# One pack of h, transposed through DRAM and in squares of 32 instead of by TensorE, in a two-layer graph kernel

## The chip, the cores and the metric

The kernel runs on one core of a Trainium2 chip. A core has five engines with queues of their own: TensorE (PE in the profile; its weight loads are listed apart as PEld), VectorE (DVE), ScalarE (ACT), GpSimd (POOL) and SyncE (SP). Here SP and ACT issue the DMAs, and sixteen DMA engines carry them. The metric is device time in microseconds, the median of several executions; lower is better. Kernel before: 2154.19 us, the median of three runs from 2152.48 to 2154.23.

## The reference: what is computed

`x` is 3327 x 512 and `adj` 3327 x 3327, all float32. Two layers follow each other, each with a residual:

```
h = relu(layernorm(x))
q, k, v = h @ Wq.T + bq, h @ Wk.T + bk, h @ Wv.T + bv
x = x + softmax(q @ k.T / sqrt(512) + adj + adj) @ v

h = relu(layernorm(x))
A2 = adj + I;  d = diag(A2) ** -0.5
x = x + relu((d[:, None] * A2 * d[None, :]) @ (A2 @ h @ W.T))
```

The kernel pads the rows to 3328, which is 26 tiles of 128 rows.

## The kernel before, in words

Queries and keys are never made apart. `Wq` and `Wk` are multiplied into one 512 x 512 matrix `M`, the first layer's scores are `h` times `M` times `h` transposed, and every large product is done as a product of 2 x 2 blocks with seven multiplications in place of eight. So TensorE needs `h` transposed, with the 512 features on the partitions, and it needs it as seven left factors: A11, A12, A22 and four sums S1 to S4.

**The packs.** The 26 row tiles are 13 pairs: tile t of the upper half and tile t of the lower half of the rows. `PACKS` (L204) divides the pairs into four packs, of 4, 3, 3 and 3 pairs, and `TURN` (L205) sets the order in which they are prepared: pack 1, 2, 0, 3. "The third pack" is pack 0: four pairs, eight tiles, 512 columns per half. `hp[k]` (L208) holds pack k: for each of the seven factors two chunks of 128 features by n x 128 columns. The upper half of the rows gives A11 (feature chunks 0 and 1) and A12 (chunks 2 and 3); the lower half gives A21 and A22, of which A21 goes only into the sums S1 = A22 + A21 and S3 = A11 + A21. S2 = S1 + A11, and S4 = A12 + S2.

**How a pack is turned.** There are two ways in the kernel before.

- `h_transposed` (L295 to L316), for the first three packs in that order. For each tile: load of 128 rows of `x` (L266), statistics on VectorE (L185 to L195) with a power on GpSimd (L191), normalisation and relu on ScalarE into a tile `ht` (L302), a store of `ht` to DRAM by rows for later use (L303), four 128 x 128 transposes on TensorE into PSUM (L306), and the way out of PSUM: one copy on ScalarE for an upper tile (L309), or a copy on ScalarE and two additions on VectorE for a lower tile (L311 to L313). At the end of a pack there are two wide additions (L315, L316).
- `Turned` (L324 to L381), for the fourth pack only. It loads the pack from a transposed copy of `x` in DRAM (L356) and applies mean and scale there; the means and scales come by way of six-row transposes on TensorE (L343), a small store (L346) and two broadcast loads (L360). The second of these loads goes into buffer `half1`.

**Rings of buffers.** `ht` comes from a ring of four buffers (`n_ring`, L262), `xt` from a ring of eleven (L261). The transposes go through two PSUM banks (L220, `tp_bank`).

**The products.** `project_q(k)` (L383) multiplies pack k by `M`: two chains (`o` = 0, 1) of seven products each. A chain (`Chain`, L222) issues m1, p5, p2, p6, then p4 of the chain before, p3, p7; its own p4 waits until the next chain. m1 reads A11, p5 reads S1, p2 reads A12, p6 reads S2, p3 reads S4, p7 reads S3, p4 reads A22. A product is two matmuls, which the profile lists as four. ScalarE (L403) and VectorE (L407) gather them into `qs`, and SP stores `qs` to DRAM (L415). After four of the seven products something else can be put beside (`place`, L391), counted from `late` on.

**What sets the order.** Within this first part of the kernel each engine's order is planned by the framework's scheduler, by the order in the program and by its own estimate of when inputs are ready. Only inside `in_order(...)` (L112) does an engine keep the order of the program among the instructions written there. Before, that is VectorE's order during the products of the third and fourth pack (L462 to L467). SP issues its DMAs one after the other, and a DMA that waits holds back all that are behind it in SP's order.

After this part come the scores (L542 to L588), the attention and the second layer (L935 above all), all tied to TensorE.

At the end of the kernel the same two building blocks that the change uses are at work already, on other data: `x1c` is filled by DMAs in runs of 128 bytes (L1154 to L1161), and VectorE transposes in squares of 32 (L1169).

Of the kernel before, what the change touches and what calls it, by code (L numbers as in the profile page):

```python
# [10 lines left out]
F32 = mybir.dt.float32  # L11
AF = mybir.ActivationFunctionType
# [3 lines left out]
P = 128  # L16
BW = 512
# [18 lines left out]
HALF = 13  # L36
# [7 lines left out]
ROW = tuple(STRIPS[s] + y * HT[s] + k for y in range(2) for s in range(2) for k in range(HT[s]))  # L44
# [3 lines left out]
def graph_layers_kernel(  # L48
# [30 lines left out]
    nc = tc.nc  # L79
    NP, D = x.shape  # L80
    DC = D // P
    NT = NP // P
    scale = 1.0 / math.sqrt(D)
# [11 lines left out]
    def half(k, shape, name):  # L95
        return arena.tile(shape, F32, name=name, tag=f"half{k}")
# [31 lines left out]
    dram = ctx.enter_context(tc.tile_pool(name="dram", bufs=1, space=bass.MemoryType.DRAM))  # L128
# [53 lines left out]
    def norm(src, kept=None):  # L182

        st = small.tile([P, 6], F32, name="st")
        nc.vector.bn_stats(st, src)  # L185
        mv = small.tile([P, 2], F32, name="mv") if kept is None else kept
        nc.vector.bn_aggr(mv, st)
        ve = small.tile([P, 1], F32, name="ve")
        nc.vector.tensor_scalar(ve, mv[:, 1:2], EPS, None, op0=ALU.add)  # L189
        rstd = small.tile([P, 1], F32, name="rstd") if kept is None else kept[:, 1:2]  # L190
        nc.gpsimd.tensor_tensor(rstd, ve, mhalf, op=ALU.pow)  # L191

        def bias():
            nb = small.tile([P, 1], F32, name="nb")
            nc.vector.scalar_tensor_tensor(nb, mv[:, 0:1], -1.0, rstd, op0=ALU.mult, op1=ALU.mult)  # L195
            return nb

        return rstd, bias
# [23 lines left out]
    class Chain:  # L222
# [7 lines left out]
        def __init__(self, product, first, more, last):  # L230


            X, Y, Z = x_bank("X"), y_bank("Y"), z_bank("Z")
            product(Y, "m1", True)
            first(0, Y, -1)
            product(Z, "p5", True)
            first(3, Z, -1)
            product(X, "p2", True)
            more(0, X)
            product(Y, "p6", False)  # L240
            first(1, Y, -1)
            Chain.finish()
            product(Z, "p3", False)
            more(1, Z)
            product(Y, "p7", False)
            more(3, Y)

            def rest():
                product(Y, "p4", False)
                first(2, Y, 1)  # L250
                last()

            Chain.before = rest
# [10 lines left out]
    def load_x(i, queue=nc.sync):  # L264
        xt = x_ring([P, D], "xt")
        queue.dma_start(xt, x[ROW[i] * P : (ROW[i] + 1) * P])  # L266
        return xt
# [27 lines left out]
    def h_transposed(k, tp_bank=tp_bank):  # L295

        a, n = PACKS[k]
        for _, i in (o for o in order if o[0] == k):
            xt = first.pop(i) if i in first else load_x(i)
            rstd, bias = norm(xt)  # L300
            ht = n_ring([P, D], "ht")
            nc.scalar.activation(ht, xt, AF.Relu, bias=bias(), scale=rstd)  # L302
            nc.sync.dma_start(rowd[0][ROW[i]], ht)  # L303
            pt = tp_bank("tp").rearrange("p (c e) -> p c e", c=DC)
            for c in range(DC):
                nc.tensor.transpose(pt[:, c], ht[:, c * P : (c + 1) * P], ident)  # L306
            w = slice((i % HALF - a) * P, (i % HALF - a + 1) * P)
            if i < HALF:
                nc.scalar.copy(hp[k][:, 0:2, :, w], pt.rearrange("p (a c) e -> p a c e", a=2))  # L309
            else:  # L310
                nc.scalar.copy(hp[k][:, 2, :, w], pt[:, 2:4])  # L311
                nc.vector.tensor_add(hp[k][:, 3, :, w], hp[k][:, 2, :, w], pt[:, 0:2])
                nc.vector.tensor_add(hp[k][:, 5, :, w], hp[k][:, 0, :, w], pt[:, 0:2])  # L313
            yield
        nc.vector.tensor_add(hp[k][:, 4], hp[k][:, 3], hp[k][:, 0])  # L315
        nc.vector.tensor_add(hp[k][:, 6], hp[k][:, 1], hp[k][:, 4])  # L316

    def after(ins, other):
# [2 lines left out]
                          mybir.DependencyInfo(mybir.DependencyClass.NoSync, mybir.DependencyReason.DATA),  # L321
                          reason="in_order")

    class Turned:  # L324


# [12 lines left out]
        def turn(self):  # L339
            k, stats, n = self.k, self.stats, PACKS[self.k][1]  # L340
            pt, by_row = tp_bank("tp"), half(3, [P, P], "by_row")
            for m in range(2):
                nc.tensor.transpose(pt[: 2 * n, m * P : (m + 1) * P], stats[:, m], ident)  # L343
                rows = by_row[32 * m : 32 * m + 2 * n]
                nc.scalar.copy(rows, pt[: 2 * n, m * P : (m + 1) * P])
                nc.sync.dma_start(normd[k][m][0, : 2 * self.w].rearrange("(i p) -> i p", p=P), rows)  # L346

        def load(self):
            k, w = self.k, self.w
            self.other = half(2, [P, 2, BW], "a21")[:, :, :w]  # L350
            a11, a12, a22 = hp[k][:, 0], hp[k][:, 1], hp[k][:, 2]
            for y, blocks in enumerate(((a11, a12), (self.other, a22))):
                c0 = ROW[y * HALF + PACKS[k][0]] * P
                xs = xT[:, c0 : c0 + w].rearrange("(z c p) e -> z p c e", z=2, p=P)
                for z, to in enumerate(blocks):
                    after(nc.sync.dma_start(to, xs[z]), self.row)  # L356
            self.norms = []
            for m in range(2):
                self.norms.append(half(m, [P, 2, BW], "norms")[:, :, :w])
                self.loaded = nc.sync.dma_start(  # L360
                    self.norms[m], normd[k][m][0:1, : 2 * w].rearrange("a (y e) -> a y e", y=2).to_broadcast([P, 2, w]))

        def parts(self):
            o, (a11, a12, a22, s1, s2, s3, s4) = self.other, (hp[self.k][:, j] for j in range(7))
            mean, by = ([e[:, y : y + 1].to_broadcast([P, 2, self.w]) for y in range(2)] for e in self.norms)
            nc.gpsimd.tensor_sub(a11, a11, mean[0])
            nc.gpsimd.tensor_sub(a12, a12, mean[0])

            def scaled(v, y):
                return nc.vector.scalar_tensor_tensor(v, v, 0.0, by[y], op0=ALU.max, op1=ALU.mult)  # L370

            yield nc.vector.tensor_sub(a22, a22, mean[1])
            yield scaled(a22, 1)
            yield nc.vector.tensor_sub(o, o, mean[1])
            yield scaled(o, 1)
            yield nc.vector.tensor_add(s1, a22, o)
            yield scaled(a11, 0)
            yield nc.vector.tensor_add(s2, s1, a11)
            yield scaled(a12, 0)
            yield nc.vector.tensor_add(s4, a12, s2)  # L380
            yield nc.vector.tensor_add(s3, a11, o)  # L381

    def project_q(k, beside=iter(()), late=0):  # L383
        a, n = PACKS[k]
        w = n * P

        qs = [half(8 + j, [P, 2, BW], "qs") for j in range(4)]

        places = itertools.count()

        def place():  # L391
            if next(places) >= late:
                next(beside, None)

        def chain(o):
            def product(ps, name, start):
                for c in range(2):
                    nc.tensor.matmul(ps[:, :w], M[B[name]][:, c, o * P : (o + 1) * P], hp[k][:, A[name], c],  # L398
                                     start=start and c == 0, stop=c == 1, skip_group_check=True)

            def first(j, ps, sign):
                d = 2 * (j % 2) + o
                nc.scalar.activation(qs[j][:, o, :w], ps[:, :w], AF.Identity, bias=u[:, d : d + 1], scale=float(sign))  # L403
                place()

            def more(j, ps):
                nc.vector.tensor_add(qs[j][:, o, :w], qs[j][:, o, :w], ps[:, :w])  # L407
                place()

            def last():  # L410
                if o == 1:
                    for j in range(4):
                        y, z = divmod(j, 2)
                        i = ROW[y * HALF + a] * P
                        ins = nc.sync.dma_start(qd[:, 2 * z : 2 * z + 2, i : i + w], qs[j][:, :, :w])  # L415
                        if behind:
                            after(ins, behind[-1])

            Chain(product, first, more, last)

        for o in range(2):
            chain(o)
# [29 lines left out]
        nc.tensor.matmul(pu[:, r : r + 1], weighed[:, r * P : (r + 1) * P], ones, start=True, stop=True)  # L452
    nc.vector.tensor_scalar(u, pu[:, :DC], scale, None, op0=ALU.mult)
    behind = []
    for then in TURN[1:3]:
        for _ in h_transposed(then):
            pass
        project_q(TURN[TURN.index(then) - 1])
    fourth = Turned(TURN[3])
    fourth.turn()  # L460
    fourth.load()
# [1291 lines left out]
```

## Time and profile before

| what | value |
|---|---|
| median of three runs | 2154.19 us |
| the profiled execution's own time | 2153.03 us |
| its span, first to last instruction | 2151.2 us |
| TensorE busy | 2137.8 us, 99% of the span |
| VectorE busy | 1653.9 us, 77% |
| ScalarE busy | 273.0 us, 13% |
| 16 DMA engines, mean over the span | 275 GB/s |
| mean granted TensorE clock | 0.998 of full speed |

The profile is of one execution. Times in it count from the start of the span. A matmul's record can overlap the next one's; the chain of work counts each stretch once. Idle time is put down to the event that ended it.

### The profile page before, as it was taken

To read this page: it belongs to the slowest core of one execution; us is meant where nothing else is said; L and a number is where in the kernel's file an instruction comes from. 1 tells how busy PE (TensorE), PEld (TensorE's weight loads), DVE (VectorE), ACT (ScalarE), POOL (GpSimd) and SP (SyncE) were. 2 spreads that over 40 slices of the span, in tenths; PEclk is the share of its full clock that TensorE was granted. 3 is DMA by queue.
4 is the path that set the end of the run, shared out by engine and by line. 5 is a ranking of instruction groups with operands and counts; after the bars stand their busy time and mean duration, and the time that the engine had idled before them with its cause. 6 is when DMAs were issued, how large, how long until landed. Compare 5 with 4: busy or idle time off the path is not lost.

```text
span 2151.2 us, 20908 instructions
## 1 busy us (share of the span) xinstructions
PE 2137.8 (99%) x6272; PEld 1182.0 (55%) x6272; DVE 1653.9 (77%) x3235; ACT 273.0 (13%) x441; POOL 68.7 (3%) x63
## 2 busy tenths in 40 slices
PE   9999999999999999999999999999999999999998
PEld 5555555555555555555454555555666665555554
DVE  7479888888997688776777778887576666778887
ACT  5312221112110000001111000000111100000000
POOL 2000000000004000000111000000000000000000
PEclk9999999999999999999999999999999999999999
DMA  8678888888999899888788889986646578978996
GB/s 301 215 241 301 303 307 286 307 293 284 328 338 293 292 370 333 280 304 304 264 304 263 308 276 369 322 310 222 198 156 209 151 219 246 313 223 245 269 288 177
DMA packets 402498, 592.10 MB, mean 275 GB/s; under 512 B 139964, under 2 KB 273480, under 8 KB 402376
## 3 DMA queue, kind: packets, MB, share of 16 engines
q1 hardware_dynamic: 374056, 532.72, 75.2%
q10 hardware_dynamic: 28320, 57.95, 7.4%
q8 instruction: 52, 0.85, 0.2%
q14 instruction: 70, 0.57, 0.1%
HBM read 422.71 MB, written 173.87 MB: 277 GB/s over the span
## 4 chain that ended last, share of the span: by engine, by line
PE 94%; DVE 3%; DMA 2%; issue 0%; ACT 0%; SPq 0%; ACTq 0%; DVEq 0%
PE p L935 55%; PE Y L542 13%; PE Z L542 6%; PE p L926 5%; PE p L1042 4%; PE pw L1103 4%; PE X L542 3%; PE Y L398 2%; PE Z L398 1%; DMA part<-sum 1%; PE X L398 1%; DMA xt<-in_x_dram 0%; DMA p<-s 0%; PE tp L306 0%; DVE g L546 0%
## 5 line engine op out<-in xcount | busy, mean ns | idle before, releaser
L935 PE MATMUL p<-part,b 128*128 128x448 f32 (+1 forms) x3528 | 1257.6, 513 | 0.3 <-DVE part L165 0.2
L935 PEld LDWEIGHTS p<-part,b 128*128 128x128 f32 x3528 | 669.9, 190 | 541.7 <-issue 290.4
L542 PE MATMUL Y<-qt,hp 128*128 128x448 f32 (+1 forms) x832 | 308.2, 513 | 0.2 <-DVE g L546 0.2
L164 DVE TENSOR_TENSOR part<-part 128x896 f32<-128x896 f32 (+1 forms) x252 | 256.8, 1019 | 65.0 <-DMA part<-p 26.2
L542 PEld LDWEIGHTS Y<-qt,hp 128*128 128x128 f32 x832 | 157.8, 190 | 133.7 <-issue 72.7
L542 PE MATMUL Z<-qt,hp 128*128 128x384 f32 (+1 forms) x416 | 162.2, 512 | 0.0
L166 DVE TENSOR_TENSOR part<-part,part 128x448 f32<-128x448 f32 (+1 forms) x219 | 129.5, 591 | 15.0
L165 DVE TENSOR_TENSOR part<-part,part 128x448 f32<-128x448 f32 (+1 forms) x219 | 129.4, 591 | 7.3
L926 PE MATMUL p<-part,b 128*128 128x448 f32 (+1 forms) x336 | 124.2, 512 | 0.0
L542 PEld LDWEIGHTS Z<-qt,hp 128*128 128x128 f32 x416 | 79.0, 190 | 66.2 <-issue 37.9
L546 DVE SCALAR_TENSOR_TENSOR g<-g,Y 128x384 f32<-128x384 f32 (+1 forms) x156 | 91.5, 587 | 30.0 <-PE Y L542 26.5
L978 ACT COPY part<-p 128x384 f32<-128x384 f32 (+1 forms) x33 | 16.6, 503 | 657.1 <-PE p L935 551.2
L926 PEld LDWEIGHTS p<-part,b 128*128 128x128 f32 x336 | 63.8, 190 | 54.1 <-issue 31.2
L549 ACT ACTIVATE g<-g 128x768 f32<-128x768 f32 (+1 forms) x48 | 43.0, 896 | 345.6 <-DVE g L546 288.0
L542 PE MATMUL X<-qt,hp 128*128 128x384 f32 (+1 forms) x208 | 81.1, 512 | 0.0
L979 DVE TENSOR_TENSOR part<-p,part 128x384 f32<-128x384 f32 (+1 forms) x33 | 19.3, 586 | 66.0 <-PE p L935 65.2
L1042 PE MATMUL p<-w,ct 128*128 128x512 f32 x136 | 61.6, 592 | 0.0
L542 PEld LDWEIGHTS X<-qt,hp 128*128 128x128 f32 x208 | 39.5, 190 | 33.1 <-issue 19.3
L191 POOL TENSOR_TENSOR rstd<-ve,mhalf 128x1 f32<-128x1 f32 x46 | 38.9, 847 | 530.6 <-DVE ve L189 502.1
L998 DVE TENSOR_TENSOR ct<-p,part 128x448 f32<-128x448 f32 (+1 forms) x72 | 42.3, 609 | 16.1 <-PE p L926 12.0
L1103 PE MATMUL pw<-w,rows 128*128 128x256 f32 x208 | 53.4, 379 | 0.0
L1033 DVE TENSOR_TENSOR job<-job 128x896 f32<-128x896 f32 (+1 forms) x52 | 52.9, 1018 | 0.0
(194 smaller groups left out, 1683.5 us busy)
## 6 DMA issues: line engine op xcount, KB each, us to landing
part<-sum SPq DMA_DIRECT2D x104, 448.0 KB, 5.0
part<-p SPq DMA_DIRECT2D x91, 448.0 KB, 5.9
part<-sum SPq DMA_DIRECT2D x104, 384.0 KB, 4.1
part<-p SPq DMA_DIRECT2D x91, 384.0 KB, 4.3
part<-in_adjT_dram SPq DMA_DIRECT2D x78, 448.0 KB, 5.1
b<-row SPq DMA_DIRECT2D x234, 128.0 KB, 4.8
part<-in_adjT_dram SPq DMA_DIRECT2D x78, 384.0 KB, 3.8
g<-in_adjT_dram SPq DMA_DIRECT2D x52, 448.0 KB, 4.2
```

Of the source, the lines that this page charges most:

```text
L164: yield nc.vector.tensor_add(o[:, 0:2], g[:, 0:4:3], g[:, 1:2].to_broadcast([P, 2, g.shape[-1]]))
L165: yield nc.vector.tensor_add(o[:, 2], o[:, 1], g[:, 0])
L166: yield nc.vector.tensor_add(o[:, 3], o[:, 2], g[:, 2])
L398: nc.tensor.matmul(ps[:, :w], M[B[name]][:, c, o * P : (o + 1) * P], hp[k][:, A[name], c], start=start and c == 0, stop=c == 1, skip_group ...
L542: nc.tensor.matmul(ps[:, :wd], h_of(self.t, name, k), qt[B[name]][:, k], start=start and k == 0, stop=k == 1, skip_group_check=True)
L546: nc.vector.scalar_tensor_tensor(a[n], a[n], 2.0, ps[:, :wd], op0=ALU.mult, op1=ALU.add if sign > 0 else ALU.subtract)
L549: nc.scalar.activation(g[1], g[1], AF.Exp, **({"bias": pad} if self.t == HALF - 1 else {}))
L926: yield nc.tensor.matmul(ps[("p2", "p3", "p4", "p8")[k]][:, :w], b[:, z], a[:, 0, y], start=k == 3 and not self.seeded, stop=True, skip_gr ...
L935: yield nc.tensor.matmul(ps[r][:, :w], b[:, i], m, start=self.t == 0 and not adds, stop=self.t == PAIRS - 1 and r in ("p1", "p5", "p6", "p ...
L1033: nc.vector.tensor_add(self.a, self.a, self.b)
L1042: nc.tensor.matmul(ps, cts[s][y][d][:, k * P : (k + 1) * P], w[d], start=d == 0, stop=d == DC - 1)
L1103: nc.tensor.matmul(ps, a, W[B[name]][:, c], start=new and c == 0, stop=c == 1, skip_group_check=True)
```

## The change

The third pack is no longer turned by `h_transposed`. A new class `Blocked` normalises its eight tiles as before, all four upper tiles first and then the lower four. It stores each `ht` twice: by rows as before, and by chunks of 128 features into a new DRAM tensor `by_chunk`. It then loads `by_chunk` back so that 128-byte runs (32 floats) of 32 rows land on 32 partitions: four loads for the upper half, eight for the lower half. After that each square of 32 x 32 still has to be transposed, which VectorE does in place, and four wide additions make the sums. The third pack's A21 is kept in the buffer `half1`. The program's order changes too: `project_q(TURN[0])` now stands before the third pack's preparation, and VectorE's share of that preparation is put beside the products of the second pack from the ninth place on (`late` is 8), in a fixed order on VectorE.

```diff
+    class Blocked:
+        def __init__(self, k):
+            self.k, (a, n) = k, PACKS[k]
+            self.rows = [dram.tile([DC, n * P, P], F32, name=f"by_chunk{y}") for y in range(2)]
+            for y in range(2):
+                for t in range(n):
+                    i = a + t + y * HALF
+                    xt = first.pop(i) if i in first else load_x(i)
+                    rstd, bias = norm(xt)
+                    ht = n_ring([P, D], "ht")
+                    nc.scalar.activation(ht, xt, AF.Relu, bias=bias(), scale=rstd)
+                    to = self.rows[y][:, t * P : (t + 1) * P]
+                    nc.sync.dma_start(to.rearrange("d p e -> p d e"), ht.rearrange("p (d e) -> p d e", d=DC))
+                    nc.sync.dma_start(rowd[0][ROW[i]], ht)
+                self.load(y)
+
+        def load(self, y):
+            k, w = self.k, PACKS[self.k][1] * P
+            if y == 0:
+                blocks = [(hp[k][:, 0:2].rearrange("p a c w -> p (a c w)"), slice(0, 4))]
+            else:
+                self.other = half(1, [P, 2, BW], "a21")[:, :, :w]
+                blocks = [(self.other.rearrange("p c w -> p (c w)"), slice(0, 2)),
+                          (hp[k][:, 2].rearrange("p c w -> p (c w)"), slice(2, 4))]
+            for to, ds in blocks:
+                rows = self.rows[y][ds].rearrange("d (j r) (a e) -> a r (d j) e", r=32, e=32)
+                for a in range(4):
+                    nc.sync.dma_start(to[32 * a : 32 * a + 32].rearrange("r (j e) -> r j e", e=32), rows[a])
+
+        def parts(self):
+            o, (a11, a12, a22, s1, s2, s3, s4) = self.other, (hp[self.k][:, j] for j in range(7))
+            def turn(v):
+                v = v.rearrange("p c w -> p (c w)")
+                return nc.vector.transpose(v, v)
+            yield turn(a11)
+            yield turn(a12)
+            yield turn(a22)
+            yield turn(o)
+            yield nc.vector.tensor_add(s1, a22, o)
+            yield nc.vector.tensor_add(s2, s1, a11)
+            yield nc.vector.tensor_add(s4, a12, s2)
+            yield nc.vector.tensor_add(s3, a11, o)
...
     behind = []
-    for then in TURN[1:3]:
-        for _ in h_transposed(then):
+    for _ in h_transposed(TURN[1]):
+        pass
+    project_q(TURN[0])
+    third = Blocked(TURN[2])
+    with in_order(nc.vector.engine):
+        parts = third.parts()
+        project_q(TURN[1], parts, 8)
+        for _ in parts:
             pass
-        project_q(TURN[TURN.index(then) - 1])
     fourth = Turned(TURN[3])
```

## The prediction, made before the changed kernel was run

> **What bounds the kernel now.** I read the page's busy table first, then the chain that ended last between 44 and 94 us, where the third pack is turned, then the instructions by form for prices, then DMA by stretches. The busy table:
>
> ```profile
> PE 2137.8 (99%) x6272; PEld 1182.0 (55%) x6272; DVE 1653.9 (77%) x3235; ACT 273.0 (13%) x441; POOL 68.7 (3%) x63
> ```
>
> TensorE leaves 13.4 us of the span. The chain around the change:
>
> ```profile
> 45.36 1.29 PE Y L398 x4
> 46.65 0.87 PE tp L306 x8
> 47.52 0.65 PE Y L398 x2
> 48.17 0.44 PE tp L306 x4
> ...
> 52.07 0.87 PE tp L306 x8
> 52.94 0.65 PE X L398 x2
> 53.59 0.65 PE Y L398 x2
> 54.24 0.58 PE tp L306 x4
> 54.82 1.94 PE Y L398 x6
> ...
> 68.36 0.11 PE tp L343
> 68.47 0.86 PE Y L398 x2
> ```
>
> From 46.65 on there is nothing but TensorE: the third pack's transposes lie between the second pack's products, and the third pack's products start at 68.47. So TensorE work taken out here shortens the kernel one to one, if the data arrive; and every microsecond by which they come late is a microsecond lost. Later stages keep TensorE as densely busy (the waits listed for it over the whole span sum to 4.5 us, 3.7 of them in the first 26), so what is won or lost here stays.
>
> VectorE and the DMA engines have room. Five-microsecond stretches (PE, PEld, DVE, ACT and POOL busy, TensorE clock, DMA share, GB/s):
>
> ```profile
> 43.00:48.00 5.00, 5.00 (x22) 3.19 (x21) 4.39 (x17) 1.86 (x5) 3.04 (x6) 1.00 0.44 164
> 48.00:53.00 5.00, 5.00 (x30) 3.75 (x29) 2.10 (x8) 5.00 (x10) 0.00 (x0) 1.00 0.89 328
> 53.00:58.00 5.00, 5.00 (x19) 2.90 (x18) 3.29 (x8) 5.00 (x10) 0.00 (x0) 1.00 0.45 166
> 58.00:63.00 5.00, 5.00 (x17) 2.92 (x16) 2.19 (x4) 2.33 (x4) 0.00 (x0) 1.00 0.98 320
> ```
>
> Prices, from the tiles `turned` and `x1c` at the kernel's end:
>
> ```profile
> L1169 DVE STREAM_TRANSPOSE turned<-part x4: 969/970/972, 1985.5 to 2108.8; 128x768 f32<-128x768 f32 x4
> L1161 SPq DMA_DIRECT2D x1c<-x1d x56: 526/527/1120, 1668.5 to 1942.7; - x56
> L1181 SPq DMA_DIRECT2D out_dram<-turned x56: 315/704/3473, 1970.1 to 2145.3; - x56
> ```
>
> **What the Trainium skill says.** "VectorE: DVE Perf Modes", The three transpose paths: VectorE turns only squares of 32, independently. The trace agrees: L1169 is paired with DMAs that place the squares. "DMA: Bandwidth & Descriptors", Two DMAs through the same engine are not ordered: a DMA that reads what another wrote must wait for that one's completion. That makes the new loads wait on SP for the stores to land; a store of `ht` takes 2.0 to 5.9 us to landing here, median 3.1. "TensorE: Matmul & The Clock Gate", Part 1 (The HAM clock gate): after an idle window of some 3.4 us TensorE's clock falls to half. The trace shows only a relative: 0.83 in 20 to 30 us, where PE is busy 7.32 of 10, and 1.00 afterwards.
>
> **Removed.** TensorE: 32 transposes, 0.87 + 3 x 0.44 + 0.87 + 0.58 = 3.64 us of chain. That is all TensorE can give: 0.17%. ScalarE: four copies of 0.594 (L309) and four of 0.387 (L311), 3.9 us. VectorE: eight additions of 0.415 (L312, L313), 3.3 us. Off the path, worth nothing unless they clear the way for another step.
>
> **Added on VectorE.** Four transposes of 128x1024. The 896- and 768-wide ones take 1.104 and 0.970, 0.134 for 128 columns, so 1.24 each; plus S1 and S3, two additions of 1.22 (L315 has that width). 7.4 us added, 4.1 net. S2 and S4 only move. From 53 to 68 us VectorE idles 8.4 of 15, so the amount is hidden, but not its position. Without the transposes the second pack's products run from 46.65 for 56 x 0.3225 = 18.06, to 64.71. The ninth place follows p2 of the second chain, which ends at 59.55. VectorE's fixed order is then: add p2 (0.55) to 60.2; A11 to 61.45; A12 to 62.7; A22 to 63.9; add p3 (0.55) to 64.5; A21 to 65.7; add p7 to 66.3; S1 to 67.5. TensorE does L343 (0.22) and m1 (1.72) from 64.71 and wants S1 at 66.65. It waits 1.05 us with the handover. S2 (68.7), S4 and S3 (71.2) are then in time. Best net result: 3.64 - 1.05 = 2.6 us.
>
> **Added on SP and the DMA engines.** Eight stores by chunk (512 runs of 512 bytes) and twelve loads, 16384 runs of 128 bytes. No row shows a load of such runs into SBUF. SP's issue: 0.53 to 0.70 us for 896 runs in L1161 and L1181. If the cost goes with the runs it is 16384 / 896 x 0.53 to 0.70 = 9.7 to 12.9 us, if with the number of DMAs 12 x 0.53 = 6.3. I take 10, plus 8 x 0.4 for the stores. DMA engines: L1161 moves 214 GB/s while alone, 9.6 ns per 128-byte run on an engine; the last stores (2130 to 2135 us) have 4782 packets at 79.6% of 16 engines, 13.3 ns. So the loads fill all engines for 16384 x 9.6 to 13.3 / 16 = 9.8 to 13.6 us. The stores are 2.1 MB: 6 us at 370 GB/s, 14 at 145. Together 16 to 28, I take 18. From 43 to 63 the free share is 0.56 + 0.11 + 0.55 + 0.02, 6 us; room comes from the fourth pack's stores and its four loads of 384 KB (L356, from 59.57), which can wait. This is the tight point.
>
> **When the data land.** As before, the first four `ht` end at 37.4. Their stores leave SP by 38.5 and land at 42.5; the upper loads go out from then to 46 and land by 50, ten before A11's turn. The last four `ht` waited for ring buffers until 47.87 before, because of the transposes; now the buffers come free as stores land, and the norms end at 42.7, so they end near 44.5. Stores out by 47, landed by 51; eight lower loads issue until 56 and land near 60.5. A22's turn needs them at 62.7. Margin: 2 us.
>
> **The moved step.** `project_q(TURN[0])` now precedes the third pack; its four `qd` stores are queued on SP ahead of the new ones or between them. Before, three of them occupied SP from 42.33 to 47.89, mostly waiting for VectorE. Behind one, the last stores by chunk and the upper loads come up to 4 us later. Behind the new loads in turn stand the fourth pack's stores and loads (needed only from 76.8 on, where GpSimd begins) and the later `qd` stores. The fourth pack's scale load goes into `half1`, so it now waits for S3, the last reader of A21: 71.2, against an issue at 71.16 to 71.7 before. No cost if S3 is punctual; if late, the fourth pack is as late, but so is TensorE.
>
> **Likeliest (0.50): in time or a microsecond late.** 2.6 less some tenths for lateness: 2.3 us less, 2153.03 - 2.3 = 2150.7 for an execution like the profiled one. That one lies 1.16 below the median, so the median goes to 2151.9. Own range 2150.5 to 2153.3.
>
> **Rival: late by what was saved (0.15).** The lower half lands at 63.4 to 69. S1 follows its landing by about 5.0 us (turns of A22 and A21, two adds, S1), so a landing at L stalls TensorE by L + 5.0 - 66.65. At L = 65.3 the 3.64 are used up. For it: SP's `qd` waits and the DMA sum above. Between -2 and +4.2: 2153 to 2158.
>
> **Rival: the round trip through DRAM becomes the bound (0.28).** Same mechanism past L = 69.6, where the stall is 8 us and the loss 4.3, 0.2%. That takes nine more than I reckon: 4 from the `qd` stores, 3 from SP at its upper price, and DMA engines at 28 us of work rather than 18. A halved clock after such a stall would add a few. 2158.5 to 2170, middle 2162. Against it: the lower loads would have to take as long as the whole upper half does from `ht` to landing.
>
> **Rival: more than the transposes (0.07).** Over 4.3 us needs something beyond TensorE's 3.64, such as a better plan in the first 26 us, where nearly all its idle time lies. Nothing there is edited: 2149.
>
> **The numbers.** The range takes in the likeliest case, the second and the first half of the third: 2150.2 to 2163. About 0.2%, 4.3 us, is what a measurement of this kernel can tell from no change (three runs spread by 1.75 us), so the first two cases count as no change: faster 0.07, same 0.65, slower 0.28.
>
> **What would show it.** TensorE should have 48 L306 transposes and the second pack's products in one piece of about 18 us. Right: one gap near 66 us, about 1 us, ended by VectorE's S1. If VectorE's idle time before the transposes of A11 or A22 ends with the DMA of `by_chunk`, the second or third case holds, and the gap's length is the price. New STREAM_TRANSPOSE rows should read 1.24 us, the loads' issues on SP 0.5 to 1.4. Wrong would be: the loads placed behind the fourth pack on SP, TensorE's order changed so that it waits elsewhere, or a second gap near 90 us for the fourth pack's factors.

## The result: 18.5 us slower, and the profile after

The changed kernel takes 2172.47 us in the median of six executions (2171.61 to 2173.89); the kernel before, run beside it, 2153.99 us. The ratio is 1.0086, with a 95% interval from 1.0076 to 1.0096. The forecast of 2151.9 us was wrong, and the time lies 9.5 us above the end of its range.

The transposes did go. The first line of the busy table of the kernel after has 32 matmuls fewer; but the span is 2170.5 us, so TensorE now leaves 27.4 us of it, where it left 13.4.

```profile
PE 2143.1 (99%) x6240; PEld 1181.8 (54%) x6240; DVE 1658.8 (76%) x3233; ACT 270.1 (12%) x433; POOL 69.5 (3%) x63
```

Where the time went is found by following one landmark. The first product of the scores (L542 before, L594 after) starts at 110.5 us before and at 128.6 us after. These 18.1 us are nearly the whole difference of the two spans (19.3); what follows takes 1.2 us longer. The kernel after, in stretches cut at TensorE's gaps (columns as in the prediction: PE, PEld, DVE, ACT and POOL busy, TensorE clock, DMA share, GB/s; a DMA share above 1 means that the recorded times of the packets on one engine overlap):

```profile
53.60:56.30 2.70, 0.20 (x2) 0.02 (x1) 0.04 (x1) 0.65 (x2) 0.00 (x0) 1.00 0.95 246
56.30:60.80 4.50, 4.50 (x8) 2.20 (x8) 0.51 (x1) 0.40 (x1) 0.00 (x0) 0.62 1.44 149
60.80:64.75 3.95, 0.02 (x1) 0.00 (x0) 0.00 (x0) 0.63 (x2) 0.00 (x0) 0.85 1.22 292
64.75:71.00 6.25, 6.25 (x11) 3.50 (x12) 3.03 (x8) 1.47 (x3) 0.55 (x1) 0.55 0.78 282
97.40:102.90 5.50, 0.08 (x1) 0.00 (x0) 3.21 (x3) 0.00 (x0) 3.24 (x2) 0.84 1.00 353
102.90:112.50 9.60, 8.14 (x13) 3.68 (x14) 9.57 (x12) 0.69 (x1) 1.04 (x1) 0.56 0.56 178
```

Three stretches in which TensorE stands are each followed by one in which it works at little more than half clock. The gaps are 2.50, 3.94, 0.59, 5.45 and 1.43 us, 13.9 together. The clock costs 4.50 x 0.38 + 6.25 x 0.45 + 8.14 x 0.44 = 8.1 us. Less the 3.64 us of transposes that is 18.4, against 18.1 seen. The agreement is closer than it should be: in its one traced execution the kernel before had lost 2.3 us of its own before the third pack. Its clock reads 0.50 from 26 to 28 us, and the sixteenth matmul of its products starts at 34.05 us, that of the kernel after at 31.74. Counted from there the loss is 20.4 us, and the sum leaves 2.0 of it open.

What ended the gaps is in TensorE's order of time (last bracket: idle time before, and what ended it):

```profile
56.28 4.54 PE L445 MATMUL Y<-hp,M 128*128 128x384 f32 x8 [2.50 <-ACT qs L450]
64.75 2.93 PE L445 MATMUL Y<-hp,M 128*128 128x384 f32 x4 [3.94 <-ACT qs L450]
...
102.93 3.78 PE L445 MATMUL Y<-hp,M 128*128 128x512 f32 x4 [5.45 <-DVE qs L454]
108.14 2.93 PE L445 MATMUL Z<-hp,M 128*128 128x384 f32 x4 [1.43 <-DVE hp L423]
```

None is the gap that the prediction had drawn, VectorE's S1 near 66 us. The first two wait for ScalarE to empty a PSUM bank into `qs`. Why ScalarE was late is in the chain that ended last (start, length, what):

```profile
49.74 4.16 DMA by_chunk<-ht
...
58.05 0.94 SPq L353
59.03 0.84 SPq L353
59.97 4.05 DMA qd<-qs
64.12 0.59 ACT qs L450
64.75 2.29 PE Y L445 x4
...
91.80 0.47 SPq L407
92.38 8.23 DMA norms<-norm
```

Before, this chain was nothing but TensorE from 46.65 on. Now it runs through SP: the twelve loads of `by_chunk` (L353), then a store of `qs`, then ScalarE, then TensorE. Later it runs through the loads of the fourth pack's means and scales (L407). SP's queue of the kernel after shows both:

```profile
39.92 5.76 SPq L353 DMA_DIRECT2D hp<-by_chunk  x4
45.72 2.05 SPq L338 DMA_DIRECT2D by_chunk<-ht  x1
...
53.99 2.54 SPq L353 DMA_DIRECT2D a<-by_chunk  x4
56.57 3.30 SPq L353 DMA_DIRECT2D hp<-by_chunk  x4
59.97 2.26 SPq L462 DMA_DIRECT2D qd<-qs  x3
62.28 4.18 SPq L266 DMA_DIRECT2D xt<-in_x_dram  x6
```

**First cause, as the traces suggest it.** `qs` lives in four buffers (`half(8)` to `half(11)`) for every pack. The second pack's gathering may write into them only when the first pack's four `qd` stores have read them. One of these stores leaves SP at 51.23, behind the four upper loads, and three at 59.97 to 62.23, behind all twelve. The kernel before had the same wait: ScalarE's waits between 40 and 125 us show it, at the price of 5.1 us off the path.

```profile
ACT qs L403 <- DMA qd<-qs: 5.1, 2, 3.4
```

After, the same row reads 13.4 us in three, longest 7.4.

**Second cause.** The fourth pack's loads of `x` stand behind the third's loads too: 62.28 to 66.46, before 36.35 to 40.08. Its statistics, its norms (issued at 91.80, before at 71.16) and its factors are late one after the other. This is the gap at 97.4.

The third pack itself was not waited for: VectorE's turn of A11 started at 71.7 us without a wait for `by_chunk`.

### The profile page after: what moved, and what is told of

Read it like the earlier page. It is cut to its first block, busy times and chain, and to the rows that moved or that the text cites. A ratio compares the mean times of both kernels' runs of the same rounds, so it can differ in the third digit from the quotient of the medians.

```text
span 2170.5 us, 20850 instructions
## 1 busy us (share of the span) xinstructions
PE 2143.1 (99%) x6240; PEld 1181.8 (54%) x6240; DVE 1658.8 (76%) x3233; ACT 270.1 (12%) x433; POOL 69.5 (3%) x63
## 3 DMA queue, kind: packets, MB, share of 16 engines
q1 hardware_dynamic: 394856, 536.92, 75.8%
## 4 chain that ended last, share of the span: by engine, by line
PE 92%; DMA 3%; DVE 2%; SPq 1%; issue 1%; ACT 0%; POOL 0%; ACTq 0%; DVEq 0%
PE p L987 55%; PE Y L594 13%; PE Z L594 6%; PE p L978 5%; PE p L1094 4%; PE pw L1155 4%; PE X L594 3%; DMA part<-sum 1%; PE Y L445 1%; SPq L353 1%; PE Z L445 0%; DMA norms<-norm 0%; DMA qd<-qs 0%; DMA sum<-job 0%; DVE st L185 0%
## 5 line engine op out<-in xcount | busy, mean ns | idle before, releaser
L594 PE MATMUL Y<-qt,hp 128*128 128x448 f32 (+1 forms) x832 | 308.7, 513 | 0.5 <-DVE g L598 0.4
L594 PEld LDWEIGHTS Y<-qt,hp 128*128 128x128 f32 x832 | 157.7, 190 | 134.5 <-issue 72.6
L594 PE MATMUL Z<-qt,hp 128*128 128x384 f32 (+1 forms) x416 | 162.3, 513 | 0.0
L594 PEld LDWEIGHTS Z<-qt,hp 128*128 128x128 f32 x416 | 79.1, 190 | 66.1 <-issue 37.9
L978 PEld LDWEIGHTS p<-part,b 128*128 128x128 f32 x336 | 63.9, 190 | 54.1 <-issue 31.5
L594 PE MATMUL X<-qt,hp 128*128 128x384 f32 (+1 forms) x208 | 81.2, 513 | 0.0
L1031 DVE TENSOR_TENSOR part<-p,part 128x384 f32<-128x384 f32 (+1 forms) x33 | 19.3, 585 | 63.8 <-PE p L987 63.1
L445 PE MATMUL Y<-hp,M 128*128 128x384 f32 (+1 forms) x128 | 54.6, 561 | 12.0 <-ACT qs L450 6.4
L594 PEld LDWEIGHTS X<-qt,hp 128*128 128x128 f32 x208 | 39.6, 190 | 33.1 <-issue 19.3
```

Of the source, the lines that this page charges most:

```text
L594: nc.tensor.matmul(ps[:, :wd], h_of(self.t, name, k), qt[B[name]][:, k], start=start and k == 0, stop=k == 1, skip_group_check=True)
L978: yield nc.tensor.matmul(ps[("p2", "p3", "p4", "p8")[k]][:, :w], b[:, z], a[:, 0, y], start=k == 3 and not self.seeded, stop=True, skip_gr ...
```

## The experiments

My theory, called Q in the expectations, is SP's queue: the loss comes from what stands behind the new DMAs, namely the stores that free the `qs` buffers and the fourth pack's loads. The rivals are the prediction's own (the third pack arrives late), the short runs by themselves (SP held and DMA engines kept busy), and VectorE's fixed order. All times are medians, and what an edit gives back is reckoned from each kernel's distance to its own runs of the kernel before, which for the change is 18.5 us. "Before" is the kernel before, run beside each group: 2153.18 us for the first four, 2153.74 for the next four, 2153.24 for the three after, 2153.90 for the last.

### Own gathering buffers for the second pack

```diff
-        qs = [half(8 + j, [P, 2, BW], "qs") for j in range(4)]
+        if k == TURN[1]:
+            qs = [take(j, [P, 2, 3 * P], "qs") for take, j in ((half, 12), (half, 13), (mid, 4), (mid, 5))]
+        else:
+            qs = [half(8 + j, [P, 2, BW], "qs") for j in range(4)]
```

The second pack's `qs` then waits for no store. One of the buffers comes out of the ring of `xt`, which has ten left.

> The second pack's products gather into four buffers of their own, so they need not wait until the first pack's are stored. Theory Q (what is queued behind the new DMAs on SP decides: first the qd stores that free the gathering buffers, then the fourth pack's loads): TensorE's two gaps at 53.6 and 60.8 us (2.5 + 3.9 us idle, some 6 us more at half clock) vanish, 8 to 12 of the 18.5 us come back, 2160 to 2165 us; the second stall near 100 us stays. Theory A (the prediction's third case: the third pack's own factors arrive late): no change, 2172 us, TensorE waits as long at the third pack's first products.

Measured: 2165.92 us (2165.52 to 2166.36), 1.0057 [1.0040, 1.0074]. TensorE's gaps at 53.6 and 60.8 are gone; what is left in this kernel is

```profile
69.41 1.48 PE L448 MATMUL Y<-hp,M 128*128 128x384 f32 x2 [2.30 <-DVE qs L457]
...
93.26 3.58 PE L448 MATMUL Y<-hp,M 128*128 128x512 f32 x4 [4.49 <-DVE qs L457]
100.08 2.72 PE L448 MATMUL Z<-hp,M 128*128 128x384 f32 x4 [3.24 <-DVE hp L423]
```

The distance to before is 12.7 us. So 5.7 us of the loss were the buffers, less than the 8 to 12 expected, because behind that stall a smaller one comes to light at 69.4. It is VectorE's order: the last of the lower loads, issued at 60.12, had landed 4.4 us later, but the first addition for the third pack stands before the turn of A22 and waits for TensorE.

```profile
65.48 0.69 DVE L457 TENSOR_TENSOR qs<-qs,X 128x512 f32<-128x512 f32 x1 [5.74 <-issue]
66.08 1.24 DVE L360 STREAM_TRANSPOSE hp<-hp 128x1024 f32<-128x1024 f32 x1
```

### The fourth pack's loads of x ahead of the third's stores

```diff
+            own = {i: load_x(i) for i in (a + t + y * HALF for y in range(2) for t in range(n))}
+            self.later = {i: load_x(i) for k, i in order if k == TURN[3]}
             for y in range(2):
                 for t in range(n):
                     i = a + t + y * HALF
-                    xt = first.pop(i) if i in first else load_x(i)
+                    xt = own[i]
```

`Turned` takes its tiles from `later`. The third pack's own eight loads of `x` move ahead with them.

> The fourth pack's six loads of x stand ahead of the third pack's stores and loads on SP. Theory Q: the second stall (97.4 to 102.9 us and 106.7 to 108.1 us, with some 4 us at half clock after it) goes and the first stays: 2160 to 2165 us, the scales' load lands 10 us or more earlier than 99.7. Theory A: no change, 2172 us.

Measured: 2166.02 us, 1.0061 [1.0044, 1.0077]. The gap at 97 is gone, those for `qs` stay; together they have grown from 6.44 to 8.70 us (5.32 and 3.38):

```profile
60.84 4.93 PE L447 MATMUL Y<-hp,M 128*128 128x384 f32 x8 [5.32 <-ACT qs L452]
69.14 2.93 PE L447 MATMUL Y<-hp,M 128*128 128x384 f32 x4 [3.38 <-ACT qs L452]
```

12.8 us over before: the second edit gives back 5.6 us by itself, a little less than was expected.

### Both repairs

The two edits above together.

> Both repairs at once: four gathering buffers of their own for the second pack, and the fourth pack's loads of x ahead of the third pack's DMAs. Alone they gave 12.7 and 12.9 us over before, of 18.5. If they mend two separate stalls, the losses mended add up: 2153.2 + 18.5 - 5.8 - 5.6 = 2160 us, 2158 to 2162. If what is left is the arrival of the third pack's factors, the remaining gap of TensorE ends with VectorE's transposes or sums.

Measured: 2155.81 us (12 executions, 2154.43 to 2159.82), 1.0012 [1.0004, 1.0021]. Of the 18.5 us 16.4 are gone, more than the sum of the two (11.3). Each repair alone leaves gaps of 4.5 to 5.3 us, with work at the lower clock behind them, and the first gap for `qs` even grew in the one and a new one of 2.30 came up in the other. What remains in the main is VectorE's lateness with the lower half of the third pack, and TensorE's wait behind it:

```profile
66.19 0.69 DVE L459 TENSOR_TENSOR qs<-qs,X 128x512 f32<-128x512 f32 x1 [2.33 <-DMA hp<-by_chunk]
67.01 1.25 DVE L362 STREAM_TRANSPOSE hp<-hp 128x1024 f32<-128x1024 f32 x1
```

```profile
70.34 1.65 PE L450 MATMUL Y<-hp,M 128*128 128x384 f32 x2 [2.53 <-DVE qs L459]
```

Here is the prediction's own rival, the third pack arriving late, though this trace does not separate it from VectorE's order: the addition that stands before A22's turn waits for TensorE's X too, which ends within 0.1 us of the landing named here. The last experiment has the turn first and settles it. And VectorE is late not only with S1: TensorE waits for its part of the second pack's `qs`, which stands between the turns.

### The repair of the buffers in the kernel before

The first edit alone, on the kernel before.

> The kernel before, with only the second pack's own gathering buffers. If the 6.6 us that this repair gave the changed kernel were a gain of its own, the kernel before would gain several us too: about 2148. My theory: before, the stores of qs had no new DMAs ahead of them and ScalarE's waits for them (5.1 us in three) were hidden but for some tenths, so 2153.0 to 2154.5, the same as before within 0.05%.

Measured: 2152.23 us, 0.9993 [0.9984, 1.0002]. The repair gives the kernel before no gain that can be told from none; the 5.7 us were a debt of the change (the expectation has 6.6, the plain difference of two medians). Its one trace is 3.0 us ahead of that of before at the first product of the scores all the same (107.5 against 110.5), and all of it at the sixteenth matmul of the products (31.1 against 34.05). No trace but that of before has the low clock there. Whether the shorter ring of `xt` or chance makes the difference was not tried, and at the end of the kernel only 1.0 us of it shows, with an interval from 0.4 us slower to 3.4 us faster. The second edit was not tried on the kernel before; there the fourth pack's loads already leave at 36.35 to 40.08.

### Long runs instead of 128-byte runs

```diff
-                rows = self.rows[y][ds].rearrange("d (j r) (a e) -> a r (d j) e", r=32, e=32)
+                rows = self.rows[y][ds].rearrange("d n e -> (d n e)").rearrange("(a r f) -> a r f", a=4, r=32)
                 for a in range(4):
-                    nc.sync.dma_start(to[32 * a : 32 * a + 32].rearrange("r (j e) -> r j e", e=32), rows[a])
+                    nc.sync.dma_start(to[32 * a : 32 * a + 32], rows[a])
```

The same bytes by the same number of DMAs, but the values land in the wrong places. First on the change as it is:

> The twelve loads move the same bytes with the same waits, in runs of 8 KB and 4 KB instead of 128 bytes; the third pack's values therefore land in the wrong places. Theory B (the short runs keep the DMA engines and with them SP busy for 16 us): the loads need some 6 us, the qd stores go out 8 to 10 us earlier, 2156 to 2163 us. If the round trip's waits and the number of DMAs decide and not the runs: 2170 to 2173 us.

Measured: 2167.54 us, 1.0069 [1.0053, 1.0086]. That is between the two expectations. SP is held 8.0 us by the twelve loads (2.18 + 4.01 + 1.81) instead of 11.6, and 2.5 of the 8.0 pass in a wait between two of them (49.1 to 51.55); only 4.1 us of the loss go. One gap of 4.70 us ended by ScalarE's `qs` and two of 3.56 and 3.23 for the fourth pack are still there: the queue costs most of it even when every load in it is quick. Then with both repairs:

> Both repairs, and the twelve loads in long runs (8 and 4 KB; the third pack's values land in the wrong places). The difference from the two repairs alone is the price of the short runs once nothing else is behind them on SP: theory B gives 3 to 8 us less, 2151 to 2157 us; if what is left is waits of the round trip, the same time as with short runs.

Measured: 2151.58 us (20 executions, 2149.11 to 2154.44), 0.9990 [0.9983, 0.9997]; 2.2 us less than before. TensorE's gaps from 44 to 130 us in this kernel are two:

```profile
82.10 1.99 PE L450 MATMUL Y<-hp,M 128*128 128x512 f32 x4 [1.26 <-DVE qs L459]
88.27 1.53 PE L450 MATMUL Y<-hp,M 128*128 128x384 f32 x4 [0.76 <-DVE hp L419]
```

3.64 - 1.26 - 0.76 = 1.6 us; the prediction's best case had 2.6, with one gap of 1.05. The 2.2 us (interval 0.6 to 3.7) are not all the exchange's: of the 3.4 us by which this trace is ahead of that of before at the first product of the scores (107.1 against 110.5), 2.5 are there at the sixteenth matmul of the products (31.5 against 34.05), as in the kernel before with the first edit. From there on it gains 0.9 us. So the exchange of TensorE's transposes for VectorE's squares is worth some 1 to 2 us if nothing stands behind the loads and they are quick. With both repairs the short runs cost 2155.81 - 2151.58 = 4.2 us: the gap of 2.53 and, after it, from 70 to 74 us, 3.66 us of work at a clock of 0.57, which is 1.6 more.

### The traffic without the change

The kernel before, its transposes on TensorE kept. It only adds the eight stores and the twelve loads, into buffers that nobody reads at that time.

```diff
+            if k == TURN[2]:
+                to = copies[i // HALF][:, (i % HALF - a) * P : (i % HALF - a + 1) * P]
+                nc.sync.dma_start(to.rearrange("d p e -> p d e"), ht.rearrange("p (d e) -> p d e", d=DC))
             nc.sync.dma_start(rowd[0][ROW[i]], ht)
...
+                rows = copies[y][ds].rearrange("d (j r) (a e) -> a r (d j) e", r=32, e=32)
+                for a in range(4):
+                    nc.sync.dma_start(to[32 * a : 32 * a + 32].rearrange("r (j e) -> r j e", e=32), rows[a])
```

> The kernel before with TensorE's transposes kept, and the eight stores by chunk and twelve loads in runs of 128 bytes added, into buffers that are not read. Theory Q and B: the added DMAs alone do the harm, so the time is about that of the changed kernel plus the 3.6 us of transposes that it saved, 2168 to 2178 us. Theory A: nothing waits for the loads, so 2154 to 2157 us.

Measured: 2165.90 us, 1.0058 [1.0041, 1.0075]: 12.7 us lost with nothing gained, less than its expectation has (2168 to 2178 us). SP stands at the loads from 53.92 to 69.25; the fourth pack's DMAs come after them, the second pack's four stores of `qs` leave only from 79.69 on, and ScalarE and TensorE wait for them:

```profile
88.79 1.27 ACT L415 ACTIVATE qs<-Y,u 128x512 f32<-128x512 f32 x2 [12.98 <-DMA qd<-qs]
```

```profile
89.53 3.78 PE L410 MATMUL Y<-hp,M 128*128 128x512 f32 x4 [10.24 <-ACT qs L415]
```

TensorE's and VectorE's work is that of before, so a loss of this size needs neither VectorE's fixed order nor the squares. That they are not its cause in the changed kernel the version with both repairs and long runs shows, which has both and no loss. The gap sits one pack later, since here the loads are issued later.

### Other queues for the loads

```diff
-                    nc.sync.dma_start(to[32 * a : 32 * a + 32].rearrange("r (j e) -> r j e", e=32), rows[a])
+                    nc.scalar.dma_start(to[32 * a : 32 * a + 32].rearrange("r (j e) -> r j e", e=32), rows[a])
```

On the change as it is:

> The changed kernel with its twelve loads issued on ScalarE's queue instead of SP's. The DMAs, their bytes and their waits are the same, but the qd stores and the fourth pack's loads no longer stand behind them. Theory Q (SP's order): at least half of the loss comes back, 2156 to 2163 us; ScalarE's own copies may now stand behind the loads. Theory A (the third pack's factors are late) and theory B (the DMA engines are full of short runs, whoever issues them): 2168 to 2173 us.

Measured: 2167.05 us, 1.0065 [1.0048, 1.0082]. The time lies outside what theory Q allowed and just under what the rivals did; the trace tells them apart, since SP is free and ScalarE stands instead:

```profile
64.74 6.29 ACTq L353 DMA_DIRECT2D hp<-by_chunk  x4
71.07 1.05 ACT L450 ACTIVATE qs<-Y,u 128x384 f32<-128x384 f32 x2 [10.41 <-DMA hp<-by_chunk]
```

With both repairs:

> Both repairs, and the twelve loads on ScalarE's queue. Theory Q: nothing waits on SP behind the loads any more, so only the third pack's arrival and the 1 us of VectorE's order can cost something: 2151 to 2157 us. If the DMA engines themselves are the limit (theory B), no better than the two repairs alone, about 2160 us.

Measured: 2162.50 us, 1.0039 [1.0024, 1.0053], 6.7 us worse than from SP and above both expectations. The four upper loads hold ScalarE 10.97 us, 4.5 of them a wait until the first of the four had landed (49.4), the eight lower ones 7.06, and TensorE waits 8.5 us for `qs`. With both repairs and GpSimd (`nc.gpsimd`) as the issuer:

> Both repairs, and the twelve loads in runs of 128 bytes issued by GpSimd, whose queue has little else than the small powers of the norms. If what is left of the price (4.2 us against long runs) is SP's being held, 2152 to 2154. If it is the time of the DMA engines, 2155 to 2157, as from SP. If GpSimd is as slow at making such runs as ScalarE's queue was (11 us for four loads), the fourth pack's norms wait behind them on GpSimd and the second stall comes back: 2159 to 2163.

Measured: 2162.05 us, 1.0043 [1.0027, 1.0060], 8.8 us over before. GpSimd's time line:

```profile
45.66 4.36 POOL L355 DMA_DIRECT2D hp<-by_chunk  x4
57.58 3.11 POOL L355 DMA_DIRECT2D a<-by_chunk  x4 [7.56 <-DMA qd<-qs]
60.67 3.12 POOL L355 DMA_DIRECT2D hp<-by_chunk  x4
63.81 1.09 POOL L191 TENSOR_TENSOR stats<-ve,mhalf 128x1 f32<-128x1 f32 x2
```

It needs 4.36 us for the four upper loads, where ScalarE's queue needed 6.4 without its wait, but the lower loads start no sooner than from SP (57.58 against 57.38), and TensorE has a gap of 4.75 us ended at 74.71. The profile names stores of `qs` as what the lower loads waited for; why, I did not find out. The last two powers of the fourth pack's statistics stand behind the loads too, at 63.81, and the loads of its norms are out on SP at 79.8 us, 4 later than from SP (75.8).

### Short runs in the stores instead of the loads

With both repairs, each tile goes out in four DMAs of 512 runs of 128 bytes, and the loads read runs of 2 KB.

```diff
-                    nc.sync.dma_start(to.rearrange("d p e -> p d e"), ht.rearrange("p (d e) -> p d e", d=DC))
+                    for j in range(4):
+                        nc.sync.dma_start(self.rows[y][:, :, 4 * t + j], ht[32 * j : 32 * j + 32].rearrange("r (c e) -> r c e", e=32))
```

> Both repairs, and the 128-byte runs moved from the loads to the stores: each tile is stored by four DMAs of 512 such runs, the loads then read runs of 2 KB. If the short runs cost because they are read into SBUF while SP's turn-taking holds the loads back, the loads are nearly as quick as in the version with misplaced values: 2151.5 to 2153, and this would be the quickest version with all values in place. If it is the number of runs wherever they are, 16384 of them keep the DMA engines as long, and 32 stores in place of 8 hold SP: 2155 to 2158.

Measured: 2166.42 us, 1.0062 [1.0045, 1.0078], worse than both cases of the expectation. 32 stores at about 0.65 us, with the stores by rows and the upper loads between them, hold SP from 35 to 69.4 us; the lower loads leave only at 70.36, and now the third pack is truly late:

```profile
77.63 1.25 DVE L362 STREAM_TRANSPOSE hp<-hp 128x1024 f32<-128x1024 f32 x1 [3.70 <-DMA hp<-by_chunk]
```

```profile
65.58 3.36 PE L450 MATMUL Y<-hp,M 128*128 128x512 f32 x4 [2.74 <-DVE hp L362]
80.96 1.65 PE L450 MATMUL Y<-hp,M 128*128 128x384 f32 x2 [8.26 <-DVE qs L459]
```

This is the third case of the prediction, the round trip as the bound, met with its price: the turn of A22 begins 10.6 us later than with both repairs alone (77.6 against 67.0), and the kernel 11.1 us further from before (13.2 against 2.1).

### All stores before the first load

In the version with both repairs the last three stores by chunk stand behind the upper loads. Here the loads follow all eight:

```diff
-                self.load(y)
+            for y in range(2):
+                self.load(y)
```

> Both repairs with the 128-byte runs, but all eight tiles are stored before the first load. In the version with both repairs the last three stores by chunk, ready from 45 us on, stood behind the four upper loads (43.7 to 49.7 on SP), so the lower loads were issued only at 57.4 to 63.3 and VectorE waited 2.3 us for them; TensorE then stood 2.5 us and ran at half clock for some microseconds. If the short runs cost only through that lateness, the lower loads now go out some 4 us sooner, the stall goes, and this gives 2151.5 to 2153, at or a little below the kernel before (2153.5). If the short runs cost by themselves (VectorE or TensorE slowed, or DMA engines busy for others), it stays at 2155 to 2156.5. If the upper half now comes late for A11 (loads until some 54), 2157 or more.

Measured: 2156.38 us, 1.0014 [1.0008, 1.0021]; no gain. SP now is held without a pause:

```profile
49.43 6.55 SPq L356 DMA_DIRECT2D hp<-by_chunk  x4
56.09 4.77 SPq L356 DMA_DIRECT2D a<-by_chunk  x4
60.90 3.70 SPq L356 DMA_DIRECT2D hp<-by_chunk  x4
```

Issued without a pause, the 16384 short runs hold SP 15.2 us (49.43 to 64.60), as they did in the traffic without the change (53.92 to 69.25). So the lower half is ready no sooner. A22's turn, which here stands first in VectorE's order, begins at 68.0, where it began at 67.0:

```profile
67.99 1.25 DVE L363 STREAM_TRANSPOSE hp<-hp 128x1024 f32<-128x1024 f32 x1 [4.67 <-DMA hp<-by_chunk]
```

I had reckoned with lateness in the order; it is the runs' own time. SP's hold gives 15.2 x 16 / 16384 = 14.8 ns of a DMA engine for one. From 55 to 60 us, when hardly anything else is under way, they move 132 GB/s, which is 15.5 ns for 128 bytes on an engine:

```profile
55.00:60.00 5.00, 5.00 (x17) 2.94 (x16) 0.56 (x1) 1.74 (x3) 0.00 (x0) 1.00 1.47 132
```

No version of the change with all values in place beat the kernel before.

## Why the prediction was wrong

**Removed: right in the count, and the price is only in part borne out.** 32 transposes less. With the queue repaired and the runs long, the kernel gained 2.2 us, where the prediction had 2.3; but some of this is the early lead that the kernel before has with the first edit alone, so the agreement is partly luck.

**Added on VectorE: right in size.** A turn of 128x1024 takes 1.20 to 1.25 us (predicted 1.24). The 7.4 us added were hidden. The gap for S1 near 66 us did not come in the version with both repairs and long runs: S1 was done there at 65.6 us, not 67.5, and TensorE took it at 68.0, not 66.65, because it now does the third pack's two p2 products first. The gaps of 1.26 and 0.76 us at 82 and 88 stand in its place, so the sum came out near by another route than it was worked out. (`place` is called after each of the seven products of a chain, not after four; so the ninth place is where the prediction has it.)

**Added on SP and the DMA engines: mis-sized.** The price of a run was put at 9.6 to 13.3 ns and measured 14.8 to 15.5 (the last experiment). The rows it came from show such runs written to DRAM; these are read into SBUF. The room was overrated too: a DMA share below 1 was read as free, but the share went to 1.47 while 132 GB/s moved. SP's issue was put at 10 us and read 11.6 in the change and 15.0 in the last experiment. With both repairs this term is worth the 4.2 us between short and long runs. It made the rival "late by what was saved" true for the repaired kernel, in its range (2155.81 us, of 2153 to 2158) and in the main in its mechanism: A22's turn began at 67.0, not 62.7. Its formula does not fit: 67.0 + 5.0 - 66.65 is a stall of 5.3 us, and TensorE, whose order had changed, stood 2.53 and lost 1.6 by the clock.

**The moved step: this is the step that failed.** It saw that "Behind the new loads in turn stand the fourth pack's stores and loads (needed only from 76.8 on, where GpSimd begins) and the later `qd` stores", and costed both at nothing. It looked at what the `qd` stores do to the new loads, up to 4 us, and not at what the new loads do to them. Even the first pack's four, which it had "ahead of the new ones or between them", left in between (one) and behind all (three). A store looks free, because nobody reads its data for long (the first load of `qd` leaves at 92.8 us); but four buffers wait for it. The trace of before had the row, ScalarE's `qs` waiting for `qd<-qs`, 3.4 us at the longest. For the fourth pack the date was that of its last use (76.8), not of the first step of a chain: its `x` loads went from 36 to 62 us, and behind them stand statistics, normalisation, row transposes, a store and a load whose data came 8.2 us after its issue. The two repairs give back 16.4 of 18.5 us. Of the buffers that have to come free the prediction counted only those of `ht` and `half1`.

The move itself does not exist, though the section on the change and the prediction speak of it. The loop of the kernel before (L455 to L458), written out, prepares pack 2, multiplies pack 1, prepares pack 0 and multiplies pack 2, and the changed kernel does the same. The first pack's `qd` stores stood behind the third pack's preparation in the program before as well: they are written after p4 of its second chain, and that p4 waits for the next pack's first chain. What is new is how much stands ahead of them on SP, and VectorE's fixed order.

**A halved clock "would add a few".** It took 8.1 us of the 22.0 that gaps and clock cost together. "TensorE: Matmul & The Clock Gate", Part 1 (The HAM clock gate), has the clock fall after an idle window of some 3.4 us. Here gaps of 2.17, 2.30, 2.50, 2.53 and 2.74 us in five kernels were each followed by it, lone ones of up to 1.86 us were not, and neither was one of 3.56 us (at 96.34 us, the change with long runs). In the kernel before, two gaps of 1.14 and 1.54 us close together were enough, between 20 and 26 us, in the stretch that the prediction read as "only a relative". So the length of a gap alone does not decide, and the measurement stands beside the page's figure. Gap and clock together cost 1.6 times the gaps in the change (13.9 and 8.1) and with both repairs (2.53 and 1.6), but 1.2 times in the traffic without the change (10.24 and 2.5). The low clock comes in steps: in the clock records of the kernel after it lasts 3.41, 6.83 and 10.24 us.

**The rivals.** The round trip as the bound (0.28) has the sign of the result and not its mechanism: the third pack was in time for a TensorE that was itself late. Its mechanism was met only where the stores were cut up. "a second gap near 90 us for the fourth pack's factors" was named among what would make the prediction wrong, and came; no chance had been put on it.

## What to carry to other kernels

When DMAs are added to a queue, list each DMA that now stands behind them, and for each not only who reads its data but who waits for its buffer, and how long the chain is that its data begins. A cover such as "needed only from 76.8 on" has to be counted back to the first link. If a stall is found and repaired, look at once for the next: here there were three behind each other, and only the last was one that had been predicted.

## What was not expected of the hardware

- A load in runs of 128 bytes holds its issuer: on SP 0.32 to 2.03 us for one of 1024 or 2048 runs (5.76 for the four upper ones), on ScalarE's queue 6.4 us for the same four beside a wait of 4.5, on GpSimd 4.36. "DMA: Bandwidth & Descriptors", Issuing engines are not separate DMA queues, says that the time to issue is usually small relative to the DMA itself; here, in the last experiment, SP was held 15.2 of the 18.4 us from the first issue to the last landing, and another issuer only moved the wait.
- The same 2.1 MB in long runs held SP 8.0 us in the change, 2.5 of them a wait; in short runs 11.6 to 15.2.
- Making the runs of the stores short instead of those of the loads did not help: 512 runs cost SP 0.65 us a store, and there were 32.
- The two repairs together gave 16.4 us where they gave 5.7 and 5.6 alone. What a repair is worth in a chain of stalls can't be read from trying it alone.
